# A two-layer graph attention and mixture-of-experts kernel: gate scores as dot products on VectorE, attention of layer 0 in written order from its second block, and loads and stores moved

## The chip, the cores and the metric

The kernel runs on one core of one Trainium2 chip. The metric is the device time of one execution in microseconds; several executions are made and their median is taken. One further execution is recorded by the hardware profiler, and all profile lines come from such an execution.

## The reference

There are 2708 tokens of 256 features and a 2708 x 2708 matrix of zeros and ones. Two layers follow one another; each is an attention over the neighbours that the matrix names and then a mixture of 8 experts of which each token uses its best two. Shortened to what matters:

```python
# layer 0
z = layernorm(x)
q, k, v = z @ Wq.T + bq, z @ Wk.T + bk, z @ Wv.T + bv
s = where(adj > 0, q @ k.T / 16, -9e15)
x = x + elu(softmax(s) @ v)
t = layernorm(x)
logits = t @ Wr + br                       # (2708, 8): the gate
weights, experts = normalised top 2 of softmax(logits)
x = x + sum over the two of weight * (gelu((layernorm(t) * g_e + b_e) @ W1_e + b1_e) @ W2_e + b2_e)   # hidden 1024
# layer 1
H = layernorm(x) @ W_fc + b_fc
s = where(adj > 0, (H @ w_src)[:, None] + (H @ w_dst)[None, :], -1e9)
x = x + softmax(s) @ H
x = x + a mixture of the same kind          # hidden 512
```

## The kernel before, in words

Tokens are cut into 22 rows of 128 (the last has 20). Layer 0's queries are taken in six blocks: five of 512 queries, four rows each, and a last one of 148. The whole is one pass without loops on the chip: everything is unrolled, and Python generators weave side work into the main loop.

*Main loop of layer 0's attention* (`layer0_attention`). For each block `b` and each of 22 key rows `k`, `scores` makes two products of keys with queries into one PSUM tile (L545), ScalarE takes the exponential (L557), and VectorE multiplies by the block's 0/1 mask (L560). Three keys later (`LAG = 3`) `attend` multiplies with the values, one product per query row (L609), into four accumulators. The keys past 2560 are masked differently: TensorE adds a large negative number where there is no edge, from a tile `apart` that VectorE compares from a piece of the matrix (L432), loaded by `load_apart` at key `NT - 8`, that is 14 (L427). The last key row, of 20 tokens, is done by `tail_scores` (L578, L584). `queries(b + 1)` (L529) comes at key 16.

*Masks.* `masks_of(b)` loads the adjacency of a block in five chunks of 1 MB (L394), compares (L411) and turns them (L417) into the tile `mT`. It runs one block ahead, one piece per key from key 2, and asks for a chunk when it begins with the one before. The finished `mT` is stored to `neighbours` (L694) for layer 1; the store stands at the end of its block in SP's program.

*Routing.* After a block its accumulators are copied out by `evict` (L634), and for each row a generator `finish` (L622 to L628: softmax's division, ELU, the residual) and then `Experts.route` is put on `line`. `line.step()` is called once per key; a new row starts every third call, and each `yield` is one call. `route` takes the norm's statistics (`norm_stats`, with a power on GpSimd, L257), stores the row (L1120), normalises it twice (L261: once as the experts' input, once for the gate), copies it (L1143), transposes the gate's version on TensorE (`to_columns`, L274, with a copy on ScalarE, L275), multiplies it with `wr` (L1156), adds the bias (L1160), finds the best two, counts the tokens of each expert before this row with two small products (L1188, L1189), and scatters the row to two places of `disp` by GpSimd's indirect DMA (L1207).

*Experts* (`Experts`). A chunk is 128 tokens of one expert. `place` works out which expert and which rows each of the slots has: the first 24 slots from the first 16 routed rows, the rest later. `fetch_rows` reads a chunk (L1387, L1393), `fetch_weights` an expert's packed weights by indirect DMA on GpSimd into one of four ring tiles (L1368), unless the ring tile has that expert already. `slots` runs a slot: `turned` (L1429, L1435) turns the chunk, `up` makes the first products (L1457) and GELU (L1465), `down` those of the slot before (L1473), scaled on VectorE (L1479) and scattered (L1492, L1485). Layer 0's experts begin during its last query block (`begin` at key 5). The weights that `fetch_weights` reads are first packed from HBM to HBM: `pack(e)` copies all of one expert (L1021, L1025 and small ones), and is one of the pieces of `background`, taken every fifth key from block 1 on. For layer 1 the ring's first experts are already guessed and loaded by SP (`fill`).

*Who orders what.* SP's queue, which issues nearly all direct DMAs, is in written order throughout. TensorE, ScalarE and VectorE follow the written order in layer 1, from `manual_schedule` on; in layer 0's attention and experts a scheduler with a cost model orders them at build time. GpSimd is ordered by the scheduler nearly everywhere. [...]

Of the kernel before, what the change touches and what calls it, by code (L numbers as in the profile page):

```python
# [20 lines left out]
P = 128  # L21
N = 2708
D = 256
# [81 lines left out]
def adj_ffn_kernel(ctx: ExitStack, tc: tile.TileContext, a: dict, out: bass.AP):  # L105
# [84 lines left out]
    wdst_b = load_bcast("L1_gnn_w_att", D, D)  # L190

    def load_dmajor(pool, name, n):
        t = pool.tile([P, DC, n], F32, name=f"{name}_w")
        nc.sync.dma_start(t, a[name].rearrange("(c p) n -> p c n", p=P))
        return t

    wr = const.tile([P, DC, E], F32, name="wr")
    wg = const.tile([P, DC, E], F32, name="wg")
# [10 lines left out]
    def fold_gate():  # L209
        for c in range(DC):  # L210
            junk = small.tile([P, D], F32, name="junk", bufs=1)
            nc.vector.scalar_tensor_tensor(
                junk, wfc[:, c, :D], 1.0, wdst_b,
                op0=ALU.mult, op1=ALU.mult, accum_out=wfc[:, c, VALUES : VALUES + 1],
            )
        share = routing.tile([P, DC, P], F32, name="gT", bufs=2)
# [12 lines left out]
        def times_gate(dst, src):  # L229

            turned = routing.tile([P, DC, P], F32, name="gT", bufs=2)
            to_columns(turned, src, P)
            ps = misc.tile([P, GROUP, P], F32, name="misc").rearrange("p g n -> p (g n)")
# [6 lines left out]
        for c in range(DC):  # L240
            times_gate(wfc[:, c, D:VALUES], wfc[:, c, :D])
            yield
        times_gate(bfc_gate, bfc_b)


# [107 lines left out]
    def layer0_attention(line):  # L353
        with ExitStack() as scope, ExitStack() as until_last:
# [24 lines left out]
            def masks_of(b, mT):  # L379

                b0, masks, last = b * BN, MASKS[b].words(mT), BLOCKS[b][1] < BN
                n = MASKS[b].padded // QUARTER

                def load(i):
# [4 lines left out]
                    if last:  # L389
                        nc.gpsimd.memset(adj[:, :n], 0)  # L390
# [14 lines left out]
                ahead = load(0)  # L405
                for i in range(WHOLE):
                    adj, ahead = ahead, load(i + 1) if i + 1 < WHOLE else None
                    size = n if last else GROUP
                    for h in range(0, n, size):
# [7 lines left out]
                        nc.vector.transpose(to, m.bitcast(I32))  # L417
                        yield

            def load_apart(b):  # L420

                n, rows_ = len(BLOCKS[b][2]), ROWS[BLOCKS[b][2][0]]
                adj = wide.tile([P, GROUP, REST], I32, name="adj_rest", bufs=1)
# [4 lines left out]
                else:  # L428
                    nc.gpsimd.memset(adj, 0)
                    for j, t in enumerate(BLOCKS[b][2]):  # L430
                        nc.sync.dma_start(adj[: ROWS[t], j], rest[j * P : j * P + ROWS[t]])
                nc.vector.tensor_scalar(  # L432
                    apart, adj[:, :n], 0, None, ALU.is_le, saturate=False
                )
# [37 lines left out]
            with tc.tile_pool(name="fold", bufs=1, side="right") as fold:  # L472
                wq = load_dmajor(fold, "L0_gnn_Wq", D)
                wk = load_dmajor(fold, "L0_gnn_Wk", D)
                load_x(0)
                load_x(1)
                wv = load_dmajor(wide, "L0_gnn_Wv", D)
# [3 lines left out]
                with tc.manual_schedule(  # L481
# [9 lines left out]
                    first_mask = masks_of(0, mT)  # L491
                    for _ in range(GROUP):
# [5 lines left out]
                for w in (wq, wk):  # L498
                    f = fold.tile([P, DC, D], F32, name=f"flat{len(flat)}")
# [114 lines left out]
            def finish(t, raw, total):  # L614
# [6 lines left out]
                nc.vector.tensor_scalar(neg[:r], raw[:r, :D], 0.0, None, ALU.min)  # L621
                nc.scalar.activation(neg[:r], neg[:r], AF.Exp)  # L622
# [8 lines left out]
            def evict(b, accs, total):  # L631
                for j, t in enumerate(BLOCKS[b][2]):
                    raw = rows.tile([P, VALUES + 1], F32, name="raw", bufs=6)
                    copied = (nc.scalar.copy if j % 2 else nc.vector.tensor_copy)(  # L634
                        raw[: ROWS[t], : D + 1], accs[j][: ROWS[t]]
                    )
                    if j == 0:
                        experts0.issued = copied
# [6 lines left out]
            folding = fold_gate()  # L645
            for b, (b0, nb, ts_) in enumerate(BLOCKS):
                later_mask = iter(())
                if b + 1 < len(BLOCKS):
                    mT_next = mask_of(b + 1)
                    later_mask = masks_of(b + 1, mT_next)  # L650
                for k in range(NT):
# [10 lines left out]
                    if k == (0 if b == last else NT - 8):  # L662
                        apart = load_apart(b)
# [10 lines left out]
                    if b == 1 and k % GROUP == 0:  # L674
                        next(folding, None)
                    if b == 0 and k == NT - 1:
                        sums = wide.tile([P, DC], F32, name="sums", bufs=1)
                        nc.vector.tensor_reduce(sums, sums_of, AX.X, ALU.add)
                        total = all_sum(wide, sums, wv, D, "total0")
                    if k == NT - 6 and b + 1 < len(BLOCKS):  # L680
                        g_next = queries(b + 1)
                    if k >= 2:
                        next(later_mask, None)
                    if background and b > 0 and k % 5 == 1 and (b > 1 or k > 10):
# [5 lines left out]
                    if b == last and k == LAG + 2:  # L690
                        experts0.open()
                        for _ in experts0.begin():
                            pass
                nc.sync.dma_start(neighbours[b][:], mT)  # L694
                if b < last:
                    for _ in later_mask:
                        pass
                    g, mT = g_next, mT_next
# [310 lines left out]
    def pack_weights(name, hidden, own_norm):  # L1009
# [9 lines left out]
        def pack(e):  # L1019
            to = packed[e * P : (e + 1) * P, :]  # L1020
            nc.sync.dma_start(  # L1021
                to[:, :w2].rearrange("p (c h) -> p c h", c=DC),
                a[f"{name}_W1"][e].rearrange("(c p) h -> p c h", p=P),
            )
            nc.sync.dma_start(  # L1025
                to[:, w2:b2].rearrange("p (f d) -> p f d", f=hc),
                a[f"{name}_W2"][e].rearrange("(f p) d -> p f d", p=P),
            )
            nc.sync.dma_start(to[:, b2:b1], a[f"{name}_b2"][e].partition_broadcast(P))
# [5 lines left out]
        background.extend(partial(pack, e) for e in range(E))  # L1035
        return packed, hc, w2, b2, b1, ln, row

    class Experts:
        def __init__(self, layer, hidden, packed_weights, w_gate, gate_bias, own_norm, xd, disp, early):
            self.hidden, self.packed_weights, self.own_norm = hidden, packed_weights, own_norm  # L1040
            self.w_gate, self.gate_bias, self.xd, self.disp = w_gate, gate_bias, xd, disp
# [62 lines left out]
        def route(self, t, x, logits=None):  # L1104
# [3 lines left out]
            w_gate, gate_bias = self.w_gate, self.gate_bias  # L1108
# [559 lines left out]
```

## Time and profile before

| what | us |
|---|---|
| median of three executions | 1210.22 |
| lowest, highest | 1209.47, 1211.88 |
| the profiled execution's own time | 1217.16 |
| its span, first to last instruction | 1215.5 |
| layer 0: attention | 0 to 501 |
| layer 0: experts | 501 to 817 |
| last scatter, loads of layer 1 | 817 to 840 |
| layer 1: attention | 840 to 964 |
| layer 1: experts | 964 to 1190 |
| last scatter, sum and store | 1190 to 1216 |

A row of the table by stage reads: stretch, its length, then each engine's busy time with the number of instructions, the granted clock of TensorE as a share of full speed, the mean busy share of the 16 DMA engines (it can pass 1 where transfers overlap) and GB/s. [...] A line of waits reads: engine, tile and line, what released it, microseconds in all, times, the longest. A line of the timeline reads: start, duration, engine, line, operation, operands, count; the time to the next start is what an instruction costs in a stream without holes, since ends overlap.

SP's own waits up to 505 us: 64.2 us for the last mask before the stores of `mT` (L694, five times, the longest 29.4), 56.4 us for VectorE to free an adjacency tile (L394, five times) and 15.8 us for packing ahead of adjacency (L394, six times). GpSimd waited 31.0 us (twice) for a `mT` whose store had not ended (L439).

### The profile page before, as it was taken

The numbers are of one execution on the slowest core, as the hardware profiler recorded it, in microseconds if no ns is written. First come the engines' busy times: TensorE is split into PE (matmuls) and PEld (weight loads), VectorE is DVE, ScalarE is ACT, GpSimd is POOL, SyncE is SP. The second block draws the span as 40 slices with busy tenths as digits, with TensorE's granted clock in tenths as the row PEclk, the third lists the DMA queues.
The fourth block names the chain that finished last, engine by engine and source line by source line (L and its number), as shares of the span: only waits on it lengthen the run. The fifth ranks groups of instructions, "written<-read, shape, count | busy, mean of one in ns | idle before, by whom it ended". The sixth has DMA issues, their size and how long they took to land. (4 is left out here: it accounts for less than half of the span.)

```text
span 1215.5 us, 20794 instructions
## 1 busy us (share of the span) xinstructions
PE 1145.4 (94%) x6512; PEld 924.1 (76%) x6512; DVE 566.2 (47%) x2147; ACT 431.9 (36%) x1252; POOL 416.0 (34%) x519
## 2 busy tenths in 40 slices
PE   8989999999998999999999999998999988899990
PEld 5666666666665666789999999996999977789880
DVE  5466663754645647452222222224866776322224
ACT  3222221221212222353333333333776747444440
POOL 3011021110211213253333343334645558555540
PEclk9999999999998999899999999999999999999996
DMA  9394962999969394847677955633002427555557
GB/s 200 58 181 76 194 160 88 226 209 267 221 133 219 83 192 164 276 102 219 174 222 228 352 118 154 179 95 100 1 1 76 178 62 209 168 139 132 170 179 282
DMA packets 199628, 197.11 MB, mean 162 GB/s; under 512 B 91403, under 2 KB 183012, under 8 KB 193368
## 3 DMA queue, kind: packets, MB, share of 16 engines
q1 hardware_dynamic: 172442, 109.39, 40.6%
q0 software_dynamic: 26176, 83.56, 21.8%
q10 hardware_dynamic: 894, 2.77, 0.6%
q8 instruction: 54, 0.88, 0.3%
q14 instruction: 62, 0.51, 0.1%
HBM read 252.62 MB, written 66.15 MB: 262 GB/s over the span
## 5 line engine op out<-in xcount | busy, mean ns | idle before, releaser
L1457 PEld LDWEIGHTS mm<-xe,ring 128*128 128x128 f32 x2192 | 259.7, 194 | 26.0 <-issue 11.7
L1457 PE MATMUL mm<-xe,ring 128*128 128x128 f32 x2192 | 265.6, 278 | 14.5 <-DMA ring<-L_ffn_packed,weight_row 7.1
L1473 PE MATMUL acc<-ring,hT 128*128 128x256 f32 x1096 | 254.3, 381 | 1.1 <-issue 1.1
L1465 ACT ACTIVATE hT<-mm,ring 128x128 f32<-128x128 f32 x548 | 156.6, 370 | 273.1 <-issue 168.1
L1473 PEld LDWEIGHTS acc<-ring,hT 128*128 128x128 f32 x1096 | 201.3, 191 | 26.0 <-issue 2.3
L609 PEld LDWEIGHTS acc<-v,p 128*128 128x128 f32 (+1 forms) x880 | 159.7, 190 | 65.2 <-issue 41.0
L609 PE MATMUL acc<-v,p 128*128 128x257 f32 (+1 forms) x880 | 204.6, 384 | 2.3 <-DVE p L560 1.3
L545 PE MATMUL s<-g,xnT 128*128 128x512 f32 x420 | 203.0, 603 | 0.0
L1479 DVE SCALAR_TENSOR_TENSOR y<-acc,who,bias 128x256 f32<-128x256 f32 x92 | 44.4, 482 | 339.2 <-PE acc L1473 322.9
L257 POOL TENSOR_TENSOR ln_rs<-ln_rs,minus_half 128x2 f32<-128x2 f32 x88 | 66.0, 752 | 252.0 <-DVE ln_rs L253 214.4
L1207 POOL DMA_INDIRECT disp<-row,to x88 | 90.4, 1027 | 166.2 <-DVE to L1204 58.2
L1368 POOL DMA_INDIRECT ring<-L_ffn_packed,weight_row x92 | 97.6, 1060 | 128.3 <-PE acc L1473 88.4
L557 ACT ACTIVATE p<-s 128x512 f32<-128x512 f32 x105 | 62.5, 596 | 181.4 <-PE s L545 143.0
L854 PE MATMUL acc<-parts,m 128*128 128x266 f32 x924 | 126.2, 293 | 0.0
L854 PEld LDWEIGHTS acc<-parts,m 128*128 128x128 f32 x924 | 117.1, 185 | 4.1 <-ACT raw L881 0.9
L545 PEld LDWEIGHTS s<-g,xnT 128*128 128x128 f32 x420 | 76.6, 192 | 53.8 <-issue 50.5
L560 DVE SCALAR_TENSOR_TENSOR p<-p,mT 128x512 f32<-128x512 f32 x100 | 68.4, 686 | 95.2 <-ACT p L557 93.6
L1492 POOL DMA_INDIRECT xd<-y,who x45 | 71.8, 1595 | 118.7 <-issue 70.4
L821 ACT CAST m<-mT 128x512 fp32r<-128x512 fp8e4 (+4 forms) x168 | 71.6, 475 | 11.4 <-PE acc L854 7.0
L1485 POOL DMA_INDIRECT xd<-y,who x47 | 47.1, 1002 | 23.6 <-issue 11.0
L411 DVE TENSOR_SCALAR m_rows<-adj 128x512 fp8e4<-128x512 int32 (+1 forms) x105 | 42.1, 432 | 2.0 <-DMA adj<-in_adj_dram 1.9
L417 DVE STREAM_TRANSPOSE mT<-m_rows 128x128 int32<-128x128 int32 x100 | 33.4, 393 | 0.1
(252 smaller groups left out, 1028.3 us busy)
## 6 DMA issues: line engine op xcount, KB each, us to landing
adj<-in_adj_dram SPq DMA_DIRECT2D x100, 256.0 KB
L_ffn_packed<-in_L_ffn_W_dram SPq DMA_DIRECT2D x16, 1024.0 KB
xg<-disp SPq DMA_DIRECT2D x368, 32.0 KB
L_ffn_packed<-in_L_ffn_W_dram SPq DMA_DIRECT2D x16, 512.0 KB
neighbours<-mT SPq DMA_DIRECT2D x5, 1408.0 KB
mT<-neighbours SPq DMA_DIRECT2D x5, 1408.0 KB
xin<-in_x_dram SPq DMA_DIRECT2D x42, 128.0 KB
ring<-L_ffn_packed SPq DMA_DIRECT2D x4, 1154.0 KB
```

The source lines that it names most:

```text
L257: nc.gpsimd.tensor_tensor(rs[:r, 1], rs[:r, 0], minus_half[:r], ALU.pow)
L545: nc.tensor.matmul(ps[:kr, :nb], xnT[:, c, k0 : k0 + kr], g[:, c, :nb], start=(c == 0), stop=(c == DC - 1 and k < KEYS),)
L560: nc.vector.scalar_tensor_tensor(p, p, LARGEST, mask, op0=ALU.min, op1=ALU.mult)
L609: nc.tensor.matmul(accs[j][:r], p[keys, q0 : q0 + r], v[keys, k, :], start=(k == 0), stop=(k == NT - 1),)
L821: nc.scalar.copy(m[:, : q1 - q0], MASKS[b].of_key(mTs[b], k)[:, q0 - b * BN : q1 - b * BN],)
L854: nc.tensor.matmul(acc[:r], masks[t], parts[:, k, i], start=(k == 0 and i == 0), stop=False,)
L1207: nc.gpsimd.indirect_dma_start(disp[:], bass.IndirectOffsetOnAxis(ap=to[:r, j : j + 1], axis=0), rows2[:r, j], None,)
L1368: nc.gpsimd.indirect_dma_start(w, None, packed[:], bass.IndirectOffsetOnAxis(ap=self.weight_row[:, s : s + 1], axis=0), bounds_check=E * P ...
L1457: nc.tensor.matmul(ps[:, i, :], w[:, c * hidden + f * P : c * hidden + (f + 1) * P], xe[:, c, :], start=(c == 0), stop=(c == DC - 1),)
L1465: nc.scalar.activation(hT[:, f, :], ps[:, i, :], AF.Gelu, bias=w[:, b1 + f : b1 + f + 1])
L1473: nc.tensor.matmul(ps, hT[:, f, :], w[:, w2 + f * D : w2 + (f + 1) * D], start=(f == 0), stop=(f == hc - 1),)
L1492: start = nc.gpsimd.indirect_dma_start(xd[:], at, y, None, bounds_check=N - 1, oob_is_err=False, compute_op=ALU.add)
```

## The change

- *Gate dots.* `gate_rows` loads the gate matrix `Wr` to all partitions (1 MB, at key 18 of block 0), takes the mean over the features away and stores it as `wr_rows`. For rows 0 to 15, `route` takes eight multiply-and-sum operations on VectorE (`gate_dots`) of the row with `wr_rows`, four in each of two steps, and multiplies by the norm's factor; transposes, products and the second normalisation are left out there. Later rows keep them. The copy of the row goes to ScalarE.
- *Written order.* From block 1 of layer 0's attention to the end of its experts TensorE, ScalarE and VectorE follow the written order. Further `yield`s put producer and consumer a step apart, a new row starts every fifth key (every fourth from block 4), and in the experts the next chunk is turned during a slot.
- *Adjacency.* `masks_of` asks for two chunks before it begins, and for chunk `i + 2` in chunk `i`; its first load stands at key 19 of the block before. The piece for `apart` is loaded at key 4 and compared at 14.
- *Stores later.* `mT` is stored at key 2 of the next block; the row's store in `route` comes after its gate.
- *Packing in even pieces.* A quarter of an expert (half of one for layer 1) every second key from key 9 of block 0 on.
- *Guessed ring.* SP loads three ring tiles of layer 0's experts at key 5 of the last block; the steps of `begin` are spread over keys 5 to 10, 12, 16 and 21.
- Smaller: two memsets go from GpSimd to VectorE, the first weights share a mask tile, the fold of layer 1's gate has more steps, and `background` is taken every second slot.

The diff, cut to its core:

```diff
+    def gate_rows(raw):
+        raw = raw.rearrange("p (d e) -> p d e", e=E)
+        mean = small.tile([P, E], F32, name="gate_mean", bufs=1)
+        nc.vector.tensor_reduce(mean, raw.rearrange("p d e -> p e d"), AX.X, ALU.add)
+        nc.vector.tensor_scalar(mean, mean, 1.0 / D, None, ALU.mult)
+        nc.gpsimd.tensor_tensor(
+            wr_rows, raw.rearrange("p d e -> p e d"),
+            mean.unsqueeze(2).to_broadcast([P, E, D]), ALU.subtract,
+        )
+
+    def gate_dots(lg, x, r, experts, unused):
+        for e in experts:
+            nc.vector.scalar_tensor_tensor(
+                unused, x, 1.0, wr_rows[:r, e],
+                op0=ALU.mult, op1=ALU.mult, accum_out=lg[:r, e : e + 1],
+            )
...
-    def fold_gate():
+    def fold_gate(pool):
+        wdst_b = pool.tile([P, D], F32, name="wdst_b", bufs=1)
+        nc.sync.dma_start(wdst_b, a["L1_gnn_w_att"][D : 2 * D].partition_broadcast(P))
...
# masks_of
-                ahead = load(0)
+                loaded = []
+                for i in range(2):
+                    loaded.append(load(i))
+                    yield
...
+                        if h == 0 and i + 2 < WHOLE:
+                            loaded.append(load(i + 2))
                         yield
...
# the main loop
+                line.gap = GROUP if b >= last - 1 else GROUP + 1
+                if b == 1:
+                    order0.enter_context(
+                        tc.manual_schedule(engines={PE, Activation, DVE}))
...
-                    if k == (0 if b == last else NT - 8):
-                        apart = load_apart(b)
+                    if k == (0 if b == last else GROUP):
+                        apart_adj = load_apart(b)
+                    if k == NT - 8:
+                        apart = compare_apart(*apart_adj)
...
-                    if k >= 2:
+                    if k == 0 or k >= 2:
                         next(later_mask, None)
-                    if background and b > 0 and k % 5 == 1 and (b > 1 or k > 10):
+                    if k == NT - 3:
+                        even_later = iter(())
+                        if b + 2 < len(BLOCKS):
+                            even_later = masks_of(b + 2, turned_of)
+                            next(even_later)
+                    if b > 0 and k == 2:
+                        nc.sync.dma_start(neighbours[b - 1][:], turned_of[b - 1])
+                    if background and k % 2 == 1 and b < last and (b > 0 or k > 8):
                         background.pop(0)()
...
                     if b == last and k == LAG + 2:
-                        experts0.open()
-                        for _ in experts0.begin():
-                            pass
-                nc.sync.dma_start(neighbours[b][:], mT)
+                        n = FULL_AFTER[experts0.early]
+                        guess0 = experts0.open(
+                            [i * (n // RING) * E // (n + GROUP) for i in range(AHEAD)] + [-1]
+                        )
+                        for _ in range(AHEAD):
+                            next(guess0)
+                        begin0 = experts0.begin()
...
# route
+            by_dots = own_norm and t < self.early
+            if by_dots:
+                gate_dots(dots, x[:r], r, range(E // 2), rows2[:r, 1, :D])
             yield
...
-            if own_norm:
-                self.beside_early(nc.sync.dma_start(of_tile(xd, t), x[:r]))
...
-                nc.vector.tensor_copy(rows2[:r, 1, :D], rows2[:r, 0, :D])
+                if by_dots:
+                    gate_dots(dots, x[:r], r, range(E // 2, E), rows2[:r, 1, :D])
+                nc.scalar.copy(rows2[:r, 1, :D], rows2[:r, 0, :D])
...
# slots
-                if own_norm:
-                    xe = turned(s)
-                hT, bias2 = up(w, xe, who[:, 1:2], own_norm and s < 2)
-                if s + 1 < s1 and not own_norm:
+                hT, bias2 = up(w, xe, who[:, 1:2])
+                if s + 1 < s1:
                     xe = after or turned(s + 1)
...
-                if s % 5 == 4 and background:
+                if s % 2 == 1 and background:
```

## The prediction

> **What bounds the kernel now.** I read, in this order, the page's first part, the busy times by stage, the waits of TensorE in the attention of layer 0, its timeline there, the clock around its one long wait, and VectorE's timeline. Stages are cut at the first and last instruction of each block of queries.
>
> ```profile
> PE 1145.4 (94%) x6512; PEld 924.1 (76%) x6512; DVE 566.2 (47%) x2147; ACT 431.9 (36%) x1252; POOL 416.0 (34%) x519
> ```
>
> TensorE is busy in 94% of the span; by stage (columns: PE, PEld, DVE, ACT, POOL busy, granted clock, DMA share, GB/s):
>
> ```profile
> 0.00:124.00 124.00, 112.96 (x435) 73.70 (x436) 69.30 (x234) 34.52 (x80) 20.85 (x58) 1.00 0.68 129
> 124.00:208.00 84.00, 84.00 (x350) 55.56 (x349) 48.22 (x179) 19.75 (x45) 12.58 (x21) 1.00 0.65 137
> 208.00:291.00 83.00, 82.67 (x332) 54.12 (x331) 44.33 (x163) 18.34 (x41) 12.72 (x21) 1.00 1.10 233
> 291.00:379.00 88.00, 84.31 (x328) 54.65 (x329) 49.86 (x175) 19.27 (x44) 14.18 (x22) 0.98 0.95 202
> 379.00:457.00 78.00, 77.63 (x312) 50.29 (x312) 41.70 (x151) 17.90 (x42) 15.65 (x24) 0.98 0.65 149
> 501.00:543.00 42.00, 40.55 (x268) 37.57 (x269) 26.55 (x136) 23.27 (x62) 19.04 (x22) 0.92 0.47 111
> 543.00:817.00 274.00, 274.00 (x1871) 255.69 (x1869) 61.95 (x195) 89.21 (x312) 101.00 (x76) 1.00 0.68 197
> ```
>
> Rows two to five are query blocks 1 to 4: TensorE has next to no hole, so a matmul taken out there shortens the kernel, and VectorE is busy only 184.1 of 333 us. From 543 to 817 (experts of layer 0) TensorE is full; nothing that the change does to order or transfers can gain there. What comes after 817 us the change hardly touches. The waits of TensorE from 126 to 501 us:
>
> ```profile
> PE s L552 <- DVE apart L432: 3.0, 1, 3.0
> PE acc L609 <- ACT p L557: 1.0, 2, 0.5
> PE misc L274 <- DVE xn L261: 0.7, 2, 0.4
> ```
>
> One wait of 3.0 us stands out, at the end of block 3, and the clock falls after it:
>
> ```profile
> 370.00:375.00 5.00, 2.53 (x12) 1.88 (x10) 5.00 (x15) 0.00 (x0) 3.24 (x4) 1.00 1.12 197
> 375.00:380.00 5.00, 3.97 (x13) 2.24 (x14) 1.39 (x4) 0.77 (x2) 0.18 (x1) 0.55 1.07 274
> 380.00:385.00 5.00, 5.00 (x13) 2.66 (x12) 1.36 (x2) 1.20 (x2) 0.00 (x0) 0.77 0.98 338
> ```
>
> [...] 3.0 us idle, then 0.55 and 0.77 in two slices, so some 3.4 us lost on top. [...] In the window to 375 us VectorE works without a pause on masks queued ahead of the compare that TensorE waits for. [...]
>
> **The change, part by part.**
>
> *Gate dots.* Rows 0 to 15 (a row is 128 tokens) no longer go through two transposes and two products with the 8 gate columns:
>
> ```profile
> 227.62 0.38 PE L274 MATMUL misc<-ident,xn 128*128 128x128 f32 x2
> 227.84 1.88 PE L545 MATMUL s<-g,xnT 128*128 128x512 f32 x4
> 231.29 0.51 PE L1156 MATMUL misc<-wr,gT 128*128 128x8 f32 x4
> 231.66 1.96 PE L545 MATMUL s<-g,xnT 128*128 128x512 f32 x4
> ```
>
> From start to next start they take 0.22 and 0.37 us, 0.59 a row; these 16 rows lie in windows without a hole, so 16 x 0.59 = 9.4 us go from the path. VectorE gets eight multiply-and-sums a row. The same form runs twice in the fold of the attention vector:
>
> ```profile
> 36.01 0.42 DVE L212 SCALAR_TENSOR_TENSOR junk<-wfc,L_gnn_w_att_b 128x256 f32<-128x256 f32 x1
> 36.35 0.08 DVE L212 DVE_READ_ACCUMULATOR junk<-wfc,L_gnn_w_att_b 128x1 f32 x1
> 36.47 0.42 DVE L212 SCALAR_TENSOR_TENSOR junk<-wfc,L_gnn_w_att_b 128x256 f32<-128x256 f32 x1
> ```
>
> 0.46 us from start to start, 3.7 a row, 59 in all. It loses a normalisation (0.33), a copy that goes to ScalarE (0.2) and an addition (0.08), 9.8 in all. So 184.1 + 59 - 9.8 = 233 of about 320 us, 73%. The heaviest step (ELU and sum 0.7, norm 0.6, four dots 1.8, a key's product 0.6, mask 0.6, the end of another row 0.8, all from start to start) comes to about 5 us against the 3.45 us of TensorE's step, the next to 3.4; scores are attended three steps later, some 9 us after they could be ready, which hides that backlog. If that cover were gone, each microsecond of backlog would be one of TensorE. ScalarE's copy (0.4 us a row) lies beside a ScalarE at 23%. Preparing the gate once costs a 1 MB load, a reduction and a GpSimd subtraction over 2048 floats[...]; GpSimd is 16% busy and its result is wanted some seven keys, 25 us, later: nothing on the path.
>
> *Written order from block 1, compare of the last columns eight keys early, adjacency two chunks ahead, stores later.* The wait at 375 us comes from adjacency behind a 2 MB burst of packing and from masks queued ahead of the compare. Afterwards the 296 KB for the compare are asked for at key 4 instead of 14, the compare stands before those masks, and chunks are asked for about 17 us before use. So it goes: the tail products of blocks 1, 2 and 3 start at 216.5, 298.3 and 386.6 us, periods of 81.8 and 88.3, hence 6.6 us. What is late next is TensorE's own work. Of the other waits, 0.5 (key 20 of block 2) and 0.3 (a transpose that is gone) go too.
>
> *New waits.* (a) In block 1's first step two VectorE products need a vector whose load is issued in that very step, behind 1 MB of adjacency and 1 MB of packing on SP's queue; behind them on VectorE are three products of keys and two evictions that TensorE needs about 9.3 us later. With 4.7 us of work before and between, 4.6 us of slack remain. (b) The 1 MB gate load is waited for on VectorE at block 0's end. (c) TensorE's counting products of the routing stand a full step behind VectorE. (d) At each block's start accumulators must be evicted before the next product. Such waits I cannot see now: from nothing (all covered) to 8 us (one exposed stall of 4 with its half clock); no gain is possible from an added wait. I take 1.5.
>
> *Packing in 0.5 MB pieces.* Same bytes, some 32 more DMAs on SP, where a packing issue takes 0.6 us now; SP waits 15.8 us for packing ahead of adjacency now. Worth nothing by itself beyond the stall already counted; unknown from -1 to +2.
>
> *Guessed ring.* By the reference's inputs the first 2048 tokens give experts 0, 1 and 3 to ring places 0, 1 and 2, which is what the formula guesses, so three indirect loads of 2.2 MB fetch nothing. But those land in time now: experts start 1.0 us after attention ends and wait for an eviction. Next rows are turned one slot ahead on VectorE. From 501.67 us to the start of slot 5's products at 542.68 are 41.0 us; five slots of 7.03 (from 542.68 to 549.71) and routing of four rows (4 x 0.64) make 37.7. So 3.3 us can be had at most, of which table switches of ScalarE and half a clock remain; I take 1, bounds 0 and 3.3.
>
> *Block 0* stays in the scheduler's order, with other loads: idle now 11.0 us, 3.9 of it the start. Taken 0, from -3 to +3.
>
> **Sum.** 9.4 + 6.6 + 0.8 + 1 - 1.5 = 16.3 off the profiled 1217.16: 1200.9. That execution is 6.9 us above the median of the runs, 1210.22, about one such stall. Since transfers cause the stall, I don't trust it to be in every run and count half, 3.3: 13.0 off the median, 1197.2; I forecast 1197.
>
> **Rivals.**
> *More is gained (0.17).* The stall is in every run, the experts' start is recovered whole, block 0 loses 3 of its holes: 9.4 + 6.6 + 0.8 + 3.3 + 3 - 1 = 22.1, so 1188. For it: chunks wait less; against: block 0's holes are 0.4 to 0.8 us each, behind VectorE's and ScalarE's order, not transfers.
> *A wait in place of the one removed (0.18).* (a) or (b) exceeds its slack by 4 us and halves the clock: 7.4 - 1.5 more than taken, 1203. For it: the DMA share is 1.10 and 0.95 in two blocks; against: SP runs ahead of VectorE.
> *VectorE becomes the bound: slower (0.07).* Place: blocks 1 to 4. It has (320 - 184.1 + 9.8)/16 = 9.1 us free a row, so eight dots decide from 1.14 us each, and the kernel is slower from 1.14 + 13/128 = 1.24. At 1.3 us: 128 x 0.16 = 20.5, so 1218. Against: 0.46 measured, if only twice[...].
> *TensorE's freed time all comes back as waits of the written order (0.03):* 1210.
>
> **How the numbers follow.** Forecast 0.55 (1192 to 1202). With the rivals 0.17, 0.18, 0.07, 0.03. About 0.2% (2.4 us) is what a measurement here can tell from no change. Faster 0.89, same 0.04, slower 0.07. The range, 1186 to 1206, takes in the first two rivals.
>
> **What would show it.** Right: no transposes for rows 0 to 15, block periods of about 79 us, no wait for the compare and no half clock inside attention, VectorE near 73% in blocks 1 to 4, attention's end near 485 us. Wrong: dots far above 0.46 us; a TensorE wait at block 1's first keys; waits for evictions at block starts; experts of layer 0 losing their 7.03 us a slot.

## The result, and the profile after

The median went from 1211.05 us (1208.21 to 1213.93, six executions) to 1199.18 us (1194.77 to 1202.62, six executions): 11.9 us less, 0.9899 of before with a 95% interval of 0.987 to 0.9928. The forecast was 1197 with a range of 1186 to 1206. The profiled execution of the kernel after has a span of 1195.6 us; the one before had 1215.5. These two differ by more than the medians, so stages are compared below, not totals.

The page's first part of the kernel after (engine, busy time, share of the span, instructions):

```profile
PE 1128.3 (94%) x6416; PEld 914.7 (77%) x6416; DVE 645.9 (54%) x2373; ACT 434.0 (36%) x1260; POOL 424.1 (35%) x518
```

TensorE lost 96 records, six for each of 16 rows (its two transposes are two records and its two products four), and 17.1 us of busy time; VectorE gained 79.7 us. The busy times by stage of the kernel after, cut where the tail product of each block starts (columns: PE, PEld, DVE, ACT, POOL busy, granted clock, DMA share, GB/s):

```profile
120.02:201.60 81.58, 80.95 (x323) 52.63 (x321) 62.72 (x211) 19.38 (x43) 15.38 (x17) 1.00 0.67 168
201.60:279.98 78.38, 78.38 (x302) 50.38 (x301) 62.41 (x231) 18.35 (x42) 15.46 (x22) 1.00 0.77 196
279.98:358.36 78.38, 78.38 (x302) 50.38 (x301) 62.37 (x231) 18.35 (x42) 15.14 (x21) 1.00 0.67 168
358.36:439.09 80.73, 77.92 (x303) 50.77 (x302) 58.98 (x230) 18.12 (x45) 17.14 (x24) 0.98 0.62 159
439.09:489.77 50.68, 47.20 (x270) 28.58 (x268) 34.77 (x157) 12.48 (x47) 16.24 (x26) 1.00 0.63 223
```

In rows two and three TensorE has no hole at all and VectorE is busy for 62.4 of 78.4 us. The same cuts in both kernels (at the end of block 3 of the kernel before, ten of the sixteen tail products run 4.7 us ahead of the other six; the cut is at the six, which moves time between blocks 3 and 4 only):

| stretch, us | before | after |
|---|---|---|
| start to the tail product of block 0 | 121.0 | 120.0 |
| blocks 1, 2, 3, 4, tail to tail | 84.3, 80.6, 82.5, 86.3 | 81.6, 78.4, 78.4, 80.7 |
| tail of block 4 to the first expert product | 46.9 | 50.7 |
| first expert product to the seventh slot | 48.0 | 43.4 |
| from there to the end of layer 0's experts | 276.2 | 277.5 |
| sum | 825.9 | 810.7 |
| rest | 389.6 | 384.9 |

So 15.2 us come from layer 0, 14.7 of them from blocks 1 to 4. In the rest, which the change hardly touches, TensorE's waits for layer 1's weights differ from profile to profile (7.1 us before and 6.5 after; 3.5 to 11.4 in the other profiles of this study), often with half a clock behind them (in the kernel after 0.50 from 1008.4 to 1015.2 us, where the longest of these waits, 3.2 us, lies). The rest as a whole took 382.6 to 390.9 us in those, so its 4.7 us can't be put down to the change.

TensorE's waits of the kernel after from 120 to 505 us:

```profile
PE misc L1282 <- DVE sel L1277: 3.0, 2, 2.8
PE misc L295 <- DVE xn L282: 2.1, 2, 1.6
PE mm L1551 <- DVE xe L1530: 1.2, 1, 1.2
PE s L576 <- DVE mT L595: 0.6, 1, 0.6
```

The wait for the compare is gone, and another has come: the counting product of the routing, once 2.8 us late. Its place in the timeline of the kernel after:

```profile
392.17 0.49 DVE L436 TENSOR_SCALAR m_rows<-adj 128x640 fp8e4<-128x640 int32 x1 [4.49 <-DMA adj<-in_adj_dram]
...
392.97 0.19 DVE L1254 SCALAR_TENSOR_TENSOR lg<-dots,ln_rs,L_ffn_br_b 128x8 f32<-128x8 f32 x1
...
393.88 0.17 DVE L1277 TENSOR_TENSOR sel<-hot 128x8 bf16<-128x8 f32 x1
...
394.10 0.17 PE L1282 MATMUL misc<-sel,before 128*128 128x8 bf16 x1 [2.81 <-DVE sel L1277]
```

VectorE stood 4.49 us at a mask of the last block whose chunk had not landed; SP had issued the chunk's loads from 384.88 to 390.21 us, so the last of them only 2 us before the mask began. The gate's last steps, for which the data was there, stood behind it in written order, and TensorE's product stood behind those. The clock then fell:

```profile
394.00:397.50 3.50, 3.40 (x6) 1.54 (x6) 2.99 (x10) 0.99 (x3) 0.00 (x0) 0.51 0.90 171
```

That is 1.7 us lost on top of 2.8: 4.5 us, two thirds of the 6.6 us that the removed wait had cost.

### The profile page after: what moved, and what is told of

Read it like the earlier page. It is cut to its first block, busy times and chain, and to the rows that moved or that the text cites. A ratio compares the mean times of both kernels' runs of the same rounds, so it can differ in the third digit from the quotient of the medians.

```text
span 1195.6 us, 20894 instructions
## 1 busy us (share of the span) xinstructions
PE 1128.3 (94%) x6416; PEld 914.7 (77%) x6416; DVE 645.9 (54%) x2373; ACT 434.0 (36%) x1260; POOL 424.1 (35%) x518
## 3 DMA queue, kind: packets, MB, share of 16 engines
q0 software_dynamic: 26176, 76.85, 20.3%
## 5 line engine op out<-in xcount | busy, mean ns | idle before, releaser
L591 DVE SCALAR_TENSOR_TENSOR p<-p,mT 128x512 f32<-128x512 f32 x100 | 70.8, 708 | 69.7 <-ACT p L588 69.6
L262 DVE SCALAR_TENSOR_TENSOR row<-x,wr_rows 128x256 f32<-128x256 f32 x128 | 54.5, 426 | 3.3
L1579 POOL DMA_INDIRECT xd<-y,who x47 | 46.9, 998 | 23.9 <-DVE y L1573 11.4
L1530 DVE TENSOR_SCALAR xe<-xe_raw,ring 128x128 f32<-128x128 f32 x90 | 27.5, 350 | 46.9 <-DMA ring<-L_ffn_packed,weight_row 45.9
```

What stands on the lines that cost most here:

```text
L591: nc.vector.scalar_tensor_tensor(p, p, LARGEST, mask, op0=ALU.min, op1=ALU.mult)
L1579: start = nc.gpsimd.indirect_dma_start(xd[:], at, y, None, bounds_check=2 * N - 1, oob_is_err=False)
```

## The experiments

Ratios are to the kernel before, measured beside each run on the same chip, whose median lay between 1210.0 and 1216.6 us; the kernel after has 0.9899. A hundredth is 12.1 us. The theory: time is TensorE's work plus its waits; the gate leaves TensorE's path, one stall goes, VectorE's added work has cover. The rivals: VectorE is nearly full; or the gain comes from order and loads and not from the dots.

**No dots.** `by_dots` is false for every row.

```diff
-            by_dots = own_norm and t < self.early
+            by_dots = False
```

> The kernel after, but with the gate of all 22 rows on TensorE again (transposes, two products, second normalisation); everything else of the change stays, the loading of the gate's rows too. Theory (the time is TensorE's work, and dots lie beside it): 9.4 us slower than the kernel after, about 1208.5, the blocks' periods 2.4 us longer each, and the 2.8 us stall near 391 us stays or moves. Rival (the written order and the earlier loads made the gain, dots on VectorE cost about what they free): within 3 us of the kernel after, 1199.

Measured: 0.9986 (0.9975 to 0.9998), 0.0087 or 10.5 us above the kernel after. Block 2 of this run, in the same columns:

```profile
204.10:286.09 81.99, 81.21 (x328) 52.92 (x325) 51.40 (x170) 19.82 (x46) 13.35 (x21) 1.00 0.78 187
```

Against 78.38 this is 3.6 us more: 2.83 of TensorE's work for four rows, 0.71 a row, and 0.78 of a wait for the next queries that had not been there. Over blocks 1 to 4 TensorE's busy time is 325.1 us, against 313.8 in the run with the mask pieces apart (below); the clock was 1.00 in all four blocks of both runs: 11.3 for 16 rows. The stall near 391 us is gone from this profile: TensorE reaches that key later, and the mask waits 1.8 us for its chunk instead of 4.5 without holding TensorE up. The rival falls: this interval and that of the kernel after do not touch.

**Double dots.** Every dot is issued twice.

```diff
-        for e in experts:
+        for e in [e for e in experts for _ in range(2)]:
```

> The kernel after with every dot issued twice, the second overwriting the first with the same number: 128 more dots, about 59 us more of VectorE in blocks 1 to 4 and the last one's first keys, 292 of 319 us. Theory (the dots have cover: scores are attended three keys later): the periods of the blocks keep within 2 us of 78.4 and the time within 4 us of the kernel after, 1199 to 1203. Rival (VectorE is close to the bound already): each block takes on some 4 to 8 us, 1215 to 1230.

Measured: 1.02 (1.017 to 1.0231), 36 us above the kernel after. The theory falls in this part; there is no cover for another 0.46 us a dot. The blocks take 85.0, 88.4, 86.6 and 92.8 us. Which engine is it? TensorE's waits of this run name ScalarE first:

```profile
PE s L576 <- ACT p L588: 21.0, 10, 4.4
```

and ScalarE's timeline in block 1 tells why:

```profile
161.61 0.60 ACT L588 ACTIVATE p<-s 128x512 f32<-128x512 f32 x1 [2.85 <-PE s L576]
171.88 0.41 ACT L1234 COPY row<-row 128x256 f32<-128x256 f32 x1 [9.67 <-DVE row L262]
172.19 1.08 ACT L588 ACTIVATE p<-s 128x512 f32<-128x512 f32 x2
```

The row's copy on ScalarE waited 9.67 us for the last dot on VectorE (L262), because the dots write their unused products into the very half row that the copy fills. Two exponentials stood behind the copy with their scores ready, and the score tiles are two: TensorE waited 1.96 us at 172.84. In the kernel after the same copy of that row already waits 5.75 us and the two exponentials also pile up behind it, just without reaching TensorE. ScalarE's waits of the kernel after for the dots of the 16 rows, from 120 to 440 us:

```profile
ACT row L1234 <- DVE row L262: 89.1, 16, 6.7
```

**Mask pieces apart.** The last block's masks are taken at every third key.

```diff
-                        yield
+                        yield from [None] * (3 if last else 1)
```

> The kernel after with the five mask pieces of the last block at every third key instead of every key, so that its chunks are asked for six keys ahead instead of two; TensorE's order is the same. Theory (the stall at 391 us comes from VectorE waiting in order for the last chunk with the gate's steps behind it): the 4.5 us wait of the mask for its chunk, TensorE's 2.8 us for the counting product and the half clock after it go, 4.5 us in an execution that has them; as the median of the runs perhaps half, 2 to 4.5 us faster, 1195 to 1197. Rival (the counting product is late for the sake of VectorE's own work in that step): TensorE still waits over 1.5 us for it, and the time is the same.

Measured: 0.9878 (0.9846 to 0.991), by itself not told from the kernel after. In the profile the stall and its half clock are gone as the theory said (block 4: 76.1 us at a clock of 1.00 instead of 80.7 at 0.98), but the last block took 53.5 instead of 50.7. TensorE waits there 1.71 us for a normalised row, as it waited 1.64 in the kernel after; this time the clock fell behind it. The busy times of this run from 464 us:

```profile
464.00:467.40 3.40, 1.69 (x11) 0.86 (x9) 2.53 (x9) 0.32 (x2) 2.89 (x4) 1.00 0.52 116
467.40:474.40 7.00, 7.00 (x22) 3.93 (x22) 5.79 (x29) 1.90 (x9) 2.44 (x3) 0.55 0.31 77
```

Seven microseconds at 0.55 are 3.2 us lost: most of the 4.6 us won a block earlier.

**Before, with the early compare alone.**

```diff
-                    if k == (0 if b == last else NT - 8):
-                        apart = load_apart(b)
+                    if k == (0 if b == last else GROUP): compare = load_apart(b)
+                    if k == NT - 8: apart = compare()
```

> The kernel before with one part of the change alone: the piece of adjacency for the last columns asked for at key 4 and compared at key 14; the scheduler then puts the compare some 30 to 40 VectorE instructions earlier in each block. Theory (the 3.0 us wait and its half clock come from this load standing behind packing and masks): no wait for the compare, 3.3 us (stall in half the runs) to 6.6 us (in all) faster than the kernel before, 1204.5 to 1208. Rival (the transfers are late all the same, and something else waits for them instead, the next masks): another wait of 2 to 3 us in block 3 or 4, and 1210 to 1211.

Measured: 1.0173 (1.0144 to 1.0202), 21 us slower than before; neither expected it. Up to the tail of block 4 the theory holds: no wait for the compare, 324.6 us for blocks 1 to 4 instead of 333.7. But the scheduler, given another program, ordered all that follows anew. The first weights of the experts were asked for at 501.9 us instead of 475.9, and TensorE's first wait there, from 120 to 530 us, is

```profile
PE mm L1457 <- DVE xe L1435: 20.9, 1, 20.9
```

So the stall went with the early load and compare. Which of the two it needed is not shown: every run here moves both together, and in the kernel before VectorE worked without a pause on masks from 370 to 375 us (busy for 5.00 of 5.00), just before the late compare, so its place behind them may be enough. And a part moved alone under the scheduler doesn't show the part alone. What in its costs turned the order was not followed up.

**Double dots, unused products elsewhere.** As double dots, with a tile of their own for the products.

```diff
-                gate_dots(dots, x[:r], r, range(E // 2), rows2[:r, 1, :D])
+                gate_dots(dots, x[:r], r, range(E // 2),
+                          rows.tile([P, D], F32, name="xn", bufs=4)[:r])
```

(and so for the second half)

> The doubled dots again (each dot twice, the second overwriting the first with the same number), but their unused products go to a tile of their own instead of the half row that ScalarE's copy fills; so the copy waits for the normalisation and no longer for the eighth dot. Theory (what doubling cost was ScalarE: its copy stood behind the last dot, the exponentials behind the copy, and TensorE had no third score tile): TensorE's waits for the exponential fall from 21 us to under 8, and the time from 1.02 of the kernel before to 1.00 or below. Rival (VectorE itself is full: masked products and masks come too late whatever ScalarE does): waits and time stay, 1.015 to 1.025.

Measured: 1.0005 (0.9986 to 1.0023), 23.6 us less than double dots, 12.8 more than the kernel after. The largest of TensorE's waits, with the one for the exponential last:

```profile
PE misc L1282 <- DVE sel L1277: 5.5, 4, 2.8
PE s L576 <- DVE mT L595: 4.3, 4, 1.5
...
PE s L576 <- ACT p L588: 0.8, 1, 0.8
```

21.0 us became 0.8. So about two thirds of what doubling cost was ScalarE's copy behind the dots, and one third VectorE itself, now late with the gate and the tail's masks (one of the waits for the gate, 2.8 us, is again behind a mask whose chunk was late).

**Scheduler's order.** The written order of layer 0 is taken out.

```diff
-                if b == 1:
+                if b < 0:
                     order0.enter_context(
```

> The kernel after without the written order in layer 0: TensorE, ScalarE and VectorE are ordered by the scheduler there again; dots, loads, stores, packing and guess stay. Theory (the dots are worth 10 us in any order; the written order only keeps the compare ahead of the masks and the next row's work behind the masked products): no wait for the compare since its data is there early, some small waits of TensorE for VectorE, 0 to 6 us slower than the kernel after, 0.99 to 0.995 of the kernel before. Rival (the written order is what makes room for the dots): waits of 2 us and more per row, 1.00 or slower.

Measured: 1.0069 (1.0049 to 1.0089), 20.6 us above the kernel after: the rival's number, but not its place. Blocks 1 to 4 take 320.3 us against 319.1. The loss lies behind them, in TensorE's wait for rows 16 and up (120 to 530 us):

```profile
PE misc L295 <- DVE xn L282: 12.6, 2, 9.6
```

with half a clock from 495 to 515 us (0.50 in the slices from 500 to 514 us).

**Written order from the last block on.**

```diff
-                if b == 1:
+                if b == last:
                     order0.enter_context(
```

> The kernel after with the written order from the last block on only; blocks 1 to 4 are left to the scheduler as in the run without written order, where they took 320.3 us from tail to tail against 319.1. Theory (the written order earns its 20 us in the last block and at the experts' start, and next to nothing where the prediction put it, in blocks 1 to 4): blocks 1 to 4 within 2 us of 320, the first expert product some 46 to 52 us after the last tail of block 4, as in the kernel after, and 0.989 to 0.994 of the kernel before. Rival (rows queued up by the scheduler in blocks 1 to 4 reach the last block too late, whatever orders that): the last block and the experts' start still lose 8 us or more, 0.998 to 1.007.

Measured: 0.9991 (0.9975 to 1.0008). The rival is right: 322.1 us for blocks 1 to 4, then 60.1 us instead of 50.7 up to the first expert product, with waits of 1.3, 2.1, 2.6 and 1.7 us. That work which the scheduler's order leaves to the last block is late there whatever the order fits these waits; the rows were not followed one by one.

**No guess.** The three ring tiles are not loaded ahead.

```diff
-                        guess0 = experts0.open(
-                            [i * (n // RING) * E // (n + GROUP) for i in range(AHEAD)] + [-1]
-                        )
-                        for _ in range(AHEAD):
-                            next(guess0)
+                        experts0.open()
```

> The kernel after without the guessed ring: the first three experts' weights come by indirect DMA only, after the placing, as in the kernel before; all else stays. Theory (the guess moves 6.5 MB out of the last block's end, but the steps of begin are now spread to key 21, so without it the weights land late): TensorE's first expert product waits 3 to 10 us for the ring, 0.992 to 0.998 of the kernel before. Rival (the weights land in time all the same, as they did before the change): within 2 us of the kernel after, 0.988 to 0.992.

Measured: 1.001 (0.9996 to 1.0023), 13.4 us above the kernel after, more than the theory had. TensorE's first expert product waits 12.5 us for its chunk. The profile puts VectorE's wait down to the chunk's rows; but 864 packets of direct DMAs, mostly these rows (512 a chunk), moved from 465 to 470 us, as the queues of this run in that stretch say (packets, MB, share of 16 engines):

```profile
q1 hardware_dynamic: 864, 0.17, 19.2%
```

and VectorE went on at 500.47. From 486 to 500.4 us they read

```profile
q0 software_dynamic: 354, 4.21, 71.3%
q1 hardware_dynamic: 1434, 0.91, 20.0%
```

q0 are the weights by indirect DMA. Among q1's bytes is the store of the last block's mask (437 KB, L759), issued at 486.85. In the kernel after it is issued at 484.97 and the chunk is turned at 488.74. So it is probably this store, slowed by the weights, that the turning waited for, in memory that the store still read: an inference from times and bytes, which no run here tested. The guess had moved the weights to 455 to 465 us, where the DMA engines are otherwise empty (share 0.01 in this run, 1.01 in the kernel after).

**One chunk ahead.** Adjacency is asked for one chunk ahead, as before the change.

```diff
-                        if h == 0 and i + 2 < WHOLE:
-                            loaded.append(load(i + 2))
...
+                    loaded.extend([load(i + 1)] if i + 1 < WHOLE else [])
```

> The kernel after with each chunk of adjacency asked for one chunk ahead, as in the kernel before, instead of two; all else stays. Theory (a chunk lasts four keys, 14 us, in blocks 1 to 4, which is enough for most; in the last block it lasts one key, 3.5 us, so that the stall at 391 us grows from 2.8 us to 5 to 10): 3 to 10 us slower than the kernel after, 0.992 to 0.998 of the kernel before. Rival (two ahead was of no use, since SP runs into the same buffers): the same as the kernel after.

Measured: 0.9931 (0.9912 to 0.9949), 3.9 us above the kernel after; the two intervals overlap, so the times alone do not settle it. In the profile the stall near 391 us is now 7.5 us, and the clock, halved from within it (0.50 from 392 to 400 us), is whole again only at 401 us. TensorE's largest wait of this run:

```profile
PE s L576 <- ACT p L588: 7.5, 1, 7.5
```

This profiled execution, 1210.06 us, is the slowest of the six; the others took 1199.39 to 1203.85, so a stall of this size is not in all of them.

**Packing in bursts.** Four pieces of packing at once, every eighth key.

```diff
-            background.extend(pieces)
+            background.extend(
+                lambda i=i: [p() for p in pieces[i : i + 4]] if i % 4 == 0 else None
+                for i in range(len(pieces)))
```

> The kernel after with the packing of layer 0's experts in bursts of 2 MB every eighth key instead of 0.5 MB every second; same bytes, same mean rate. Theory (the even pieces were costed at nothing, from -1 to +2 us, since adjacency is asked for two chunks ahead): within 2 us of the kernel after, 0.988 to 0.992. Rival (bursts are what makes adjacency late): a stall of 3 us or more for masks or for the counting product in blocks 2 to 4 and the last block's chunks later still, 0.993 to 1.0.

Measured: 0.9901 (0.9873 to 0.9929): the same. The stall at 391 us is 3.0 instead of 2.8 us. The even pieces are worth nothing that shows.

**All rows by dots**, with the mask pieces apart and the unused products elsewhere.

```diff
-            by_dots = own_norm and t < self.early
+            by_dots = own_norm
```

> The kernel after with three edits: the last block's mask pieces at every third key, the dots' unused products in a tile of their own, and the gate of all 22 rows by dots, so that rows 16 to 21 too send no transposes to TensorE. Theory (TensorE's work decides wherever VectorE has cover): 6 x 0.6 = 3.5 us of TensorE less and no wait of 1.7 us for a normalised row in the last block, with its half clock 3.4 us: 4 to 8 us faster than with the mask pieces alone, 0.981 to 0.985 of the kernel before. Rival (VectorE is 93% busy from 455 to 470 us, so that four more rows of dots there have no cover): TensorE waits for masked products in the last block or for the first chunk's transposes, 0.99 or slower.

Measured: 1.0008 (0.9995 to 1.0022), 13.2 us above the kernel after and 19 to 24 above what the theory expected. The rival is right. In the last block a key lasts 1.7 us, not 3.45, and a row still brings eight dots. TensorE's two largest waits, with half a clock behind both of the stretches where they lie (0.53 from 468 to 470, 0.50 from 482 to 486 and from 502 to 510 us):

```profile
PE s L576 <- ACT p_last L588: 8.3, 5, 4.3
PE mm L1551 <- DMA xg<-disp: 7.5, 1, 7.5
```

The second is again a chunk turned long after the last mask's store was issued (493.65 to 503.77 us), which fits the inference on that store above.

**Improved.** Mask pieces apart, unused products elsewhere, and one more step between norm and transposes for rows 16 to 21.

```diff
-                yield
+                yield from [None] * 2
                 to_columns(gT[:, :, :r], xt, r)
```

(the other two edits as shown above)

> The kernel after with three edits: the last block's mask pieces at every third key, the dots' unused products in a tile of their own, and one more step between the normalisation of rows 16 to 21 and their transposes. Theory (the mask edit alone left a hole of 1.7 us before a transpose in the last block, after which the clock halved and gave 3.4 us back): no hole above 1 us between 130 us and the end of attention, no half clock there, and 4 to 5 us faster than the mask edit alone in the profiled execution; 0.983 to 0.987 of the kernel before. Rival (something else is late behind it, since VectorE is behind in that stretch): another hole of 1 us or more there, and 0.987 to 0.990.

Measured: 0.9856 (0.9828 to 0.9883), median 1193.58 us, the fastest here and faster than before by 1.44%. Its interval overlaps that of the kernel after (0.987 to 0.9928), so that step is likely and not settled by the times. By the profiles 689.8 instead of 695.3 us lie between the tail of block 0 and the products that follow layer 0's experts. The time is the theory's, but its "no hole" is not. TensorE's largest waits:

```profile
PE s L576 <- ACT p_last L588: 1.9, 1, 1.9
PE mm L1551 <- ACT raw L666: 1.1, 1, 1.1
```

A hole of 1.9 us at 469 us is still followed by half a clock for 3.4 us (0.50 from 472 to 474 us). Of the 5.5 us between the profiles 4.6 come from block 4, and about 2 from layer 0's experts, at whose start the kernel after had 3.4 us of half clock (0.50 from 489.7 to 493.0 us; the first 32 records of the expert product took 5.37 us) and this one none (3.81 us); 1.3 are lost in the last block. The three edits were not run apart, so the share of the separate tile is open.

## Why the prediction was right, and where it was not

| step | predicted, us | found |
|---|---|---|
| gate leaves TensorE | 9.4 | 11.3 of work (no dots), 10.5 by the times |
| wait for the compare goes | 6.6 here, 3.3 counted | gone in every profile with the early load |
| other gaps | 0.8 | both gone |
| new waits | -1.5 (0 to -8) | -5.1 in blocks 1 to 4 |
| last block and experts' start | +1 (0 to 3.3) | -3.8 and +4.6: +0.8 |
| block 0 | 0 (-3 to +3) | +1.0 |
| even packing | 0 (-1 to +2) | 0 (bursts) |
| experts from the seventh slot on | 0 | -1.3 |

The sum was 16.3 for the profiled execution; layer 0 shows 15.2, of which 1.1 is in no row of the table. For the median it was 13.0, the runs give 11.9. That the sums come so close is in part luck: 1.9 us more from the gate and 1.0 from block 0 nearly make up for 3.6 more of new waits. Whether half a stall was the right count for the median was not tested. ScalarE's table loads, which the prediction left in place, lasted 1.28 us each, seven of them before from the first expert product to the seventh slot and nine after.

*Right for its reason:* TensorE's work sets the time of blocks 1 to 4, a dot costs 0.46 us from start to start as in the fold of the attention vector (mean 426 ns and the read), and the long stall went with the early load and compare. The gate's subtraction on GpSimd lasted 4.71 us. "Periods of about 79 us" are 78.4 in the two clean blocks, "7.03 us a slot" is unchanged, and "attention's end near 485" is 488.5. The indirect loads that the guess was to make empty show in their queue, which moved 76.85 MB instead of 83.56.

*Mis-sized:* the gate by a fifth, 0.71 us a row and not 0.59. The start-to-start times of the removed products left out that the next product of scores is slower behind them; the lines shown with the prediction have it at 1.96 us behind the gate's products and 1.88 behind a transpose, 0.08 of the missing 0.12. New waits were taken at 1.5 and are 5.1: case (c), the counting product, came true, with its half clock, behind a mask whose chunk was late; (a) and (d) show no wait of TensorE. At the place of (b) TensorE waits 0.6 us, not for the load but for the gate's reduction, 3.87 us on VectorE in front of the tail's mask; the prediction had the gate's preparation as "nothing on the path". The prediction said that chunks "are asked for about 17 us before use". That holds for whole blocks, where a chunk lasts four keys. In the last block a chunk lasts one key, so two chunks ahead are two keys, 7 us; its mask was looked at only as work, not as a load with a date. The reduction and TensorE's wait, in the timeline of the kernel after:

```profile
118.75 3.87 DVE L252 TENSOR_REDUCE gate_mean<-adj 128x8 f32<-128x2048 f32 x1
122.53 0.68 DVE L595 TENSOR_SCALAR mT<-s 128x512 fp8e4<-128x512 f32 x1
...
123.27 1.98 PE L576 MATMUL s<-g,xnT 128*128 128x512 f32 x4 [0.63 <-DVE mT L595]
```

*Wrong, though it cost nothing in the sum:* the cover. The step said that scores are attended three steps later "which hides that backlog", and the rival on VectorE that dots "decide from 1.14 us each", from VectorE's mean idle time. Doubled dots, 0.92 us each pair, lose 36 us. What gives out first is not the three steps between scores and attention but the two score tiles, because ScalarE's copy waits for the last dot. The copy was costed at 0.4 us "beside a ScalarE at 23%"; the wait that it brings, and the exponentials behind it, are in none of the four cases of its part on new waits. With the copy freed, the same doubling costs 12.8 us, which is left to VectorE. Undoubled, VectorE is busy for 77% of blocks 1 to 4 (246.5 of 319.1 us; 73% was forecast).

*Wrong in kind:* parts were priced by what each removes from the kernel before. Undone one by one in the kernel after, the dots cost 10.5 us, the guess 13.4, the written order 20.6, the second chunk 3.9 (not clear of noise) and the even pieces nothing: 48 us, for a change worth 11.9. The early compare and the later stores were not undone there. By the traces the guess and the order remove waits that the kernel before did not have (the chunk behind the weights, rows 16 and up late from VectorE), not waits of the kernel before.

*Open:* how often the stall of the kernel before, and that of the kernel after at 391 us, come up in executions without a profiler. The latter stood, with 2.8 to 3.0 us, in the profiles of the kernel after, of no guess, of bursts and of the doubled dots with a tile of their own, and not in that of no dots.

## What to carry to other kernels

Ask of each moved instruction not only what it costs but what it waits for, and what stands behind it on its engine: a throw-away output written where another engine writes next is such a wait (9.67 us here, with doubled dots). Cover is counted in the buffers between two engines and in the length of the local step, not in an engine's mean idle time, and doubling the suspected work shows in one run where it ends. An edit's worth under a written order or a scheduler is its worth beside the other edits: undo it in the finished kernel before believing its price.

## What the runs showed of the hardware

Half clock (a granted clock of 0.50) came behind some holes and not behind others. In the 14 profiles of this study the granted clock changes 152 times (worked out from slices of 1 us), and within each profile all changes lie on marks 3.413 us apart, to within 0.02 us; where the marks lie differs from profile to profile. With every profile from 120 us on cut at its own marks, the windows at full clock are:

| TensorE idle in the window | windows | followed by half clock |
|---|---|---|
| under 0.9 us | 4038 | 0 |
| 0.9 to 1.95 us | 151 | 17 |
| 1.95 us and more | 55 | 55 |

So in these profiles half clock went with TensorE's idle time within one window, not with the length of a hole. The hole of 3.0 us of the kernel before had 2.93 us in one window, and two windows of half clock followed, 6.8 us. The hole of 2.3 us in the last block of no guess was cut by a mark, with 1.9 us on one side, and had no half clock. The hole of 1.7 us in that of the mask pieces apart lay in one window, and two windows of half clock followed, 6.8 us. Ahead of the kernel after's first expert product 1.1 us in a window were enough for one. What decides in the middle row is not shown. So a hole of 1.7 us cost 1.7 us in one profile (no dots) and 5 in another (mask pieces apart).
